# An attention kernel with PSUM banks given by name and its side work ordered behind the score copies

## The chip, the cores and the metric

The kernel runs on one core of a Trainium2 chip. The metric is device time in microseconds (us) of one execution; three executions of the kernel before took 2622.65, 2625.44 and 2630.11 us, median 2625.44. Five engines work in parallel, each through its own instructions in order: PE (TensorE, matrix products into PSUM), DVE (VectorE), ACT (ScalarE), POOL (GpSimd) and SP, which here only issues DMA transfers. In the profile PEld is PE's load of weights.

## The reference

Two batches of 2048 tokens with 2048 features each, all in fp32:

```python
xn = layernorm(x)
qkv = xn @ Wqkv + bqkv                      # q, k, v of 512 features, one head
attn = softmax(q @ k.T / sqrt(512))
a = (attn @ v) @ Wo + bo
r = xn @ Wq_w.T                             # router, 16 features
gate = softmax of the top 16 of r @ keys.T, spread over 64 experts
z = (xn @ A_w.T), 64 experts of rank 8, each times its gate
out = x + a + 2 * (z @ B_w.T)
```

## The kernel before

Each fp32 operand is split into a high and a low part (`split_hi`, L121, a cast on ACT; `split_lo`, L124, a subtract on DVE), and a product is three matmuls over the parts (`PASSES`). Most products are done in the seven-product scheme of Strassen and Winograd, with steps P1 to P7 whose operands are sums of quarter blocks.

The work is staged. `first_block` transposes and normalizes the first 512 tokens (`turn`, L363 on) and makes their values; then come queries, keys and gated experts of the eight blocks of 512 tokens, four pairs of blocks in all. A block's last item makes its values (`values_out`, with DVE adds at L289, casts and subtracts, and stores `v_d<-vs`). Then attention runs from 1317.7 us to about 2010 us, and after it the output stage (`multiply`, L1408; `finish`, L1397) with 2688 matmuls.

Attention goes over four pairs of query blocks, with eight units of keys each. A unit has seven score steps, `score(g)` (L1131, six matmuls each), so a pair has 56. Their order is P1, P7, P2, P6, P4, P5 and P3, with the next unit's P1 ahead of P3 in the later pairs and after it in the first. P1's bank is copied by ACT into a further bank, U (`seed`, L1114), and then P2 adds on into P1's bank, P6, P5 and P3 into U's, and P4 into P7's. ACT copies the banks of P7, P2, P6 and P3 to SBUF (L1144, L1146, L1149, L1157); DVE adds P4 and P5 (L1151, L1154) and keeps the running maxima (`greatest`, L1100, L1103). All score banks come from one pool of seven PSUM banks, given in the order in which they are asked for (`acc`, L98); the eighth (`misc`) serves sums and spreads.

While one pair's scores are made, the pair before is weighted. `maxes` (L1166 to L1178) reduces the maxima of a block to `mq`, and `spread` (matmul L1188, copy L1192) puts them on all partitions. `soft(c)` subtracts them (L1203, DVE), takes the exponential (L1206, ACT), splits it into `ph` and keeps the sums L (L1214, L1216). `weigh(n)` multiplies `ph` by the values `vt` (L129), 64 groups of three matmuls for a block; at a block's end the sums are added over partitions by two matmuls (L1250, L1251), DVE takes the reciprocal (L1253) and multiplies the four banks by it (L1257), ACT adds the bias (L1258), and SP stores the result (L1259). The SBUF slots `ot` of that come from a ring of three of the four `mid` slots.

The order of the work is written out by hand. A table `side` deals side work to score steps: loads, splits and stores of later keys (`key_steps`: loads `kr<-k_d` at L860, casts and subtracts into `kst`, stores `kp_d<-kst`), of queries (`query_steps`, `query_load`, `query_split`, loads at L927) and of output weights (`combos`, L1288 to L1291). `key_load` (L975) loads `kt<-kp_d` four pairs of steps ahead of its score. A block `with behind("sp")` places what it holds, in the order of instructions, behind the instruction last recorded under that name. `begin` gives the step at which the weighting of each pair starts.

Of the kernel before, what the change touches and what calls it, by code (L numbers as in the profile page):

```python
# [62 lines left out]
def attn_ffn_kernel(ctx: ExitStack, tc, x, xT, wq, wv, wob, bqk, bv, bo, keysT, out):  # L63
# [31 lines left out]
    for tag, words in order:  # L95
        sb.tile([P, words], F32, name=f"slot{tag}", tag=tag, bufs=1)

    def acc():  # L98
        return psum.tile([P, T], F32, name="acc", tag="acc", bufs=7)

    def misc(shape=None):
        return psum.tile(shape or [P, T], F32, name="misc", tag="misc", bufs=1)
# [223 lines left out]
    def first_block():  # L326


        xs0 = [r_xs, r_xs, r_xs] + [big(j) for j in range(16, 21)]
        xn = [r_xh([P, 2, T], FR, "xh") for c in range(NCH)]  # L330
        rows, mv = {}, const.tile([P, NT, 2], F32, name="mv", bufs=2)
        rs = const.tile([P, NT], F32, name="rs")
        nm = const.tile([P, NT], F32, name="nm")

        def load(t, cols):
            rows[t] = [xs0[2 * t + c]([P, 1024], F32, "xs") for c in range(2)]
            for c in range(2):
                for h in range(1024 // cols):
                    a = h * cols
                    (nc.scalar if t == 0 and c else nc.sync).dma_start(  # L340
                        rows[t][c][:, a : a + cols],
                        x[t * P : (t + 1) * P, c * 1024 + a : c * 1024 + a + cols],
                    )

        def normal(t):
            st = const.tile([P, 4, 6], F32, name="st6", bufs=2)
            row_stats(mv[:, t, :], rows[t], 0, st)
            last["nm"] = nc.vector.tensor_scalar(nm[:, t : t + 1], mv[:, t, 0:1], -1.0, None, ALU.mult)
            rstd(rs[:, t : t + 1], mv[:, t, 1:2], 1)

        def scale(t):
            for n in range(4):
                c, h = divmod(n, 2)
                v = rows[t][c][:, h * 512 : (h + 1) * 512]
                if n < 3:
                    last["row"] = nc.vector.tensor_scalar(
                        v, v, mv[:, t, 0:1], rs[:, t : t + 1], ALU.subtract, ALU.mult
                    )
                else:
                    nc.scalar.activation(v, v, AF.Identity, bias=nm[:, t : t + 1])  # L360
                    last["mul"] = nc.scalar.mul(v, v, rs[:, t : t + 1])

        def turn(t, g0=0, g1=NCH // 4):  # L363
            sl = slice(t * P, (t + 1) * P)
            for g in range(g0, g1):
                pt = acc()
                for j in range(4):
                    c = 4 * g + j
                    k = (c % 8) * P
                    nc.tensor.transpose(pt[:, j * P : (j + 1) * P], rows[t][c // 8][:, k : k + P], ident)  # L370
                for part in range(2):
                    for j in range(4):
                        hi, lo = (xn[4 * g + j][:, a, sl] for a in range(2))
                        pj = pt[:, j * P : (j + 1) * P]
                        if part == 0:
                            split_hi(hi, pj)
                        else:
                            last["row"] = split_lo(lo, pj, hi)

        r_w0 = Ring(sb, "h0", "h1", "h2", "h3", "B25", "B26", "B32", "B33")  # L380

        def mul(ps, wh, t, c2):
            sl = slice(t * P, (t + 1) * P)
            for cc in range(2):
                c = 2 * c2 + cc
                product(
                    ps[:, :VH], lambda a: xn[c][:, a, sl], lambda b: wh[:, b, cc, :],
                    c == 0, c == NCH - 1,
                )

        N2 = NCH // 2
        warm = half(0)([P, T], mybir.dt.bfloat16, "warm")
        nc.vector.memset(warm, 0.0)
        pw = misc()
        for j in range(26):
            nc.tensor.matmul(pw, warm[:, :P], warm, start=True, stop=True)
        load(0, 512)
        normal(0)
        scale(0)

        wh = []

        def pieces(n):
            with behind("row", "nm", "mul"):
                while len(wh) < n:
                    eng = nc.gpsimd if 2 <= len(wh) < 5 else None
                    wh.append(wv_piece(0, len(wh), eng, ring=r_w0))

        pieces(1)
        turn(0, 0, 2)  # L410
        pieces(3)
        turn(0, 2, 4)
        pieces(5)
        load(1, 1024)
        ps = [acc() for t in range(NT)]
        for t in range(NT):
            if t + 1 < NT:
                with behind("row"):
                    normal(t + 1)
            if t == 0:  # L420
                pieces(6)
                load(2, 1024)
            for c2 in range(N2):
                if t + 1 < NT and c2 == 2:
                    scale(t + 1)
                if t == 0 and c2 == 4:
                    pieces(N2)
                    load(3, 1024)
                    constants()
                if t + 1 < NT and c2 == 6:  # L430
                    with behind("pe"):
                        turn(t + 1)
                mul(ps[t], wh[c2], t, c2)
        qr = router_in()
        for t in range(NT):
            with behind("row"):
                values_out(0, t, 0, r_ev, qr, ps[t])
        flush()
        ps = [acc() for t in range(NT)]
        for c2 in range(N2):  # L440
            w = wv_piece(1, c2)
            for t in range(NT):
                mul(ps[t], w, t, c2)
        for t in range(NT):
            values_out(0, t, 1, r_ev, qr, ps[t])
        return xn, qr
# [614 lines left out]
    r_L = half(6)  # L1061
    r_rl = half(7)
    r_ot = half(8)
    r_oo = mid(0, 1, 2)
    r_ll = mid(3)
    r_tp = mid(0, 1, 2, 3)
    r_ph = wide(0, 1, 2)
# [38 lines left out]

    bank, later = {}, []

    def seed(k):

        b = bank["U"] = acc()
        if k < 3:
            nc.tensor.matmul(b, bank["k"], bank["q"], start=True, stop=True)
        nc.scalar.copy(b, bank["P1"])  # L1114

    def score(g):

# [5 lines left out]
            bank["U0"] = bank["U"]  # L1123
        name = {"P2": "P1", "P4": "P7", "P6": "U0", "P5": "U0", "P3": "U0"}.get(step, step)
        if not more:
            bank[step] = acc()
        ps = bank[name]
        st, mv = kop.pop(g), qop[j, step]
        for d in range(2):
            for i, (a, c) in enumerate(PASSES):  # L1130
# [2 lines left out]
                    start=not more and d == 0 and i == 0, stop=d == 1 and i == 2,  # L1133
                    skip_group_check=more,
                )
        tt, copy = nc.vector.tensor_tensor, nc.scalar.copy
        if later:
            greatest(*later.pop())
        if step == "P1":
            bank["k"], bank["q"] = st[:, 0, 0, :], mv[0][:, 0, :]  # L1140
            if k < NKS:
# [2 lines left out]
            copy(unit(b1, m)[:, 1, :], ps)  # L1144
        elif step == "P2":
            copy(unit(b0, m)[:, 0, :], ps)  # L1146
            later.append((b0, m, 0))
        elif step == "P6":
            copy(S[b0, m][:, 1, :], ps)  # L1149
        elif step == "P4":  # L1150
# [2 lines left out]
        elif step == "P5":  # L1153
            tt(S[b1, m][:, 1, :], S[b1, m][:, 1, :], ps, ALU.add)  # L1154
            greatest(b1, m, 1)
        elif step == "P3":
            copy(S[b1, m][:, 0, :], ps)  # L1157
            later.append((b1, m, 0))
            if NKS <= k + 1 < NPAIR * NKS:
                seed(k + 1)  # L1160

# [31 lines left out]

    blocks = range(NB)

    def soft(c):

        if c >= NB * NK:
            return
        blk, k = blocks[c // NK], c % NK  # L1200
        u = S[blk, k // 2]
        if k % 2 == 0:
            nc.vector.tensor_tensor(  # L1203
                u, u, mbc[blk].unsqueeze(1).to_broadcast([P, 2, T]), ALU.subtract
            )
            nc.scalar.activation(u, u, AF.Exp, scale=SCALE)  # L1206
        e = u[:, k % 2, :]
        ph = r_ph([P, 2, T], FR, "ph")
        split_hi(ph[:, 0, :], e)
# [22 lines left out]
    def weigh(n):  # L1232
# [2 lines left out]
        blk, k = blocks[c // NK], c % NK  # L1235
        if d == 0:
            load_v(c + 3)
            soft(c + 2)
        if k == 0:
            av[blk, d] = acc()  # L1240
        vt, ph = vt_[c], pt_[c]
        product(
            av[blk, d], lambda a: vt[:, a, d * P : (d + 1) * P], lambda b: ph[:, b, :],
            k == 0, k == NK - 1,
        )
        if k == NK - 2 and d == 2:
            lh, ll = lsum[blk]
            with behind("pe"):
                pl = misc()
# [1 line left out]
                nc.tensor.matmul(pl, onesr, lh, start=False, stop=True)  # L1251
            rl_[blk] = r_rl([P, T], F32, "rl")
            nc.vector.reciprocal(rl_[blk], pl)  # L1253
        if k == NK - 1 and d == ND - 1:
            for d in range(ND):
                ot = r_oo([P, T], F32, "ot")
                nc.vector.tensor_tensor(ot, av[blk, d], rl_[blk], ALU.mult)  # L1257
                nc.scalar.activation(ot, ot, AF.Identity, bias=bv_sb[:, d : d + 1])  # L1258
                nc.sync.dma_start(oz_at(blk, 1, d), ot)  # L1259

# [200 lines left out]
    NW = 2 * NK * ND  # L1463
    total = NPAIR * NG1

    begin = [NG1 * (j + 1) + (9 if j in (0, NPAIR - 1) else 5) for j in range(NPAIR)]
    side = {}

    def deal(g, steps, every=1):
# [49 lines left out]
    deal(begin[0] - 8, [lambda c=c: load_v(c) for c in range(3)])  # L1519
    deal(begin[0] - 3, [lambda c=c: soft(c) for c in range(2)])  # L1520
    done = 0
    for g in range(begin[-1]):
        if g < total:
            score(g)
            if g % 2:
                key_load(g // 2 + 4)
        j, n = divmod(g, NG1)
        for st in side.get(g, []):
            with behind("sp"):
                st()  # L1530
        if j and j <= NPAIR:
            if n == 2:
                maxes(2 * j - 1)
            if n in (1, 4):
                with behind("pe"):
                    spread(2 * j - 2 + n // 4)
        if n == NG1 - 2 and j < NPAIR:
# [119 lines left out]
```

## Time and profile before

| | |
|---|---|
| three executions | 2622.65, 2625.44, 2630.11 us |
| profiled execution | 2625.36 us |
| its span | 2623.5 us |
| PE busy | 2592.8 us (99%) |
| DVE busy | 1921.8 us (73%) |
| ACT busy | 909.8 us (35%) |
| POOL busy | 528.2 us (20%) |
| moved by DMA | 608.09 MB, mean 232 GB/s |
| mean granted TensorE clock | 0.998 |

The span runs from the first to the last instruction; the execution's time has 1.9 us around it. A share is an average over all stages: DVE at 73% is nearly full in parts of attention and has room elsewhere. In the lists of waits an engine's idle time is put down to what ended it: the line and engine that released the instruction, or the DMA that landed. In a timeline a line is a group of like instructions: start, busy time, engine, line, operation, outputs and inputs, shape, number, and in brackets the idle time before the first with what ended it. A matmul of 128x128 by 128x512 starts every 0.227 us when PE works without a pause.

### The profile page before, as it was taken

Reading aid. Unit: us, or ns where it says so; the run is one execution under the profiler, and the core shown is the slowest. Engines: PE = TensorE matmul, PEld = TensorE weight load, DVE = VectorE, ACT = ScalarE, POOL = GpSimd, SP = SyncE. Lnnn points to the kernel's source line nnn. Section 1 sums busy time; section 2 is a strip of 40 time slices with the busy share of each in tenths; the row PEclk is TensorE's granted clock in tenths of the full one; section 3 lists DMA queues with packets and bytes.
Section 4 is the critical chain, followed back from the end, with each engine's and each line's share of the span. In section 5 each row is a group of like instructions: output and inputs, shape, how many; then the busy total and the mean of one; then the engine's idle time right before and its main releaser. Section 6 shows DMA issues by size and latency. Waiting matters only on the chain. (4 is left out here: it accounts for less than half of the span.)

```text
span 2623.5 us, 34496 instructions
## 1 busy us (share of the span) xinstructions
PE 2592.8 (99%) x12692; PEld 2186.1 (83%) x12692; DVE 1921.8 (73%) x2695; ACT 909.8 (35%) x1345; POOL 528.2 (20%) x318
## 2 busy tenths in 40 slices
PE   9999999999999999999989999999999999999999
PEld 8889888888888888888877887878878888888887
DVE  7567649867878677776758859678597776797775
ACT  4333223323332323343435436344264222332221
POOL 2312420001000010000000000000001665565664
PEclk9999999999999999999999999999999999999999
DMA  6767874668446683577899798899788555565542
GB/s 235 249 242 252 297 272 167 218 214 275 147 137 230 211 274 119 182 253 234 307 302 324 253 341 269 267 323 323 245 298 294 169 166 163 185 215 172 180 162 103
DMA packets 328954, 608.09 MB, mean 232 GB/s; under 512 B 27928, under 2 KB 150864, under 8 KB 328784
## 3 DMA queue, kind: packets, MB, share of 16 engines
q1 hardware_dynamic: 315824, 575.99, 65.0%
q10 hardware_dynamic: 12960, 29.89, 3.3%
q8 instruction: 100, 1.64, 0.3%
q14 instruction: 70, 0.57, 0.1%
HBM read 450.42 MB, written 155.35 MB: 231 GB/s over the span
## 5 line engine op out<-in xcount | busy, mean ns | idle before, releaser
L129 PE MATMUL acc<-t,pw 128*128 128x512 f32 x3024 | 693.7, 390 | 0.4 <-DVE pw L124 0.4
L129 PEld LDWEIGHTS acc<-t,pw 128*128 128x128 f32 x3024 | 565.4, 188 | 118.1 <-DVE pw L124 0.8
L1408 PE MATMUL acc<-wb,s 128*128 128x512 f32 x2688 | 609.4, 389 | 0.0
L1408 PEld LDWEIGHTS acc<-wb,s 128*128 128x128 f32 x2688 | 504.7, 188 | 104.6
L1392 POOL TENSOR_TENSOR xo<-xo,bo_bc 128x512 f32<-128x512 f32 x128 | 210.7, 1653 | 897.7 <-DMA vt<-v_d 605.5
L129 PE MATMUL acc<-ph,vt 128*128 128x512 f32 x1536 | 377.9, 390 | 4.5 <-DVE ot L1257 2.1
L1131 PE MATMUL acc<-qt,kt 128*128 128x512 f32 x1344 | 338.0, 393 | 14.3 <-ACT acc L1114 7.6
L129 PEld LDWEIGHTS acc<-ph,vt 128*128 128x128 f32 x1536 | 287.3, 188 | 68.4 <-DVE ot L1257 3.7
L1131 PEld LDWEIGHTS acc<-qt,kt 128*128 128x128 f32 x1344 | 252.7, 189 | 73.6 <-ACT acc L1114 8.4
L121 ACT CAST pw<-pw 128x1024 fp32r<-128x1024 f32 (+1 forms) x168 | 177.8, 1059 | 333.7 <-PE acc L129 250.2
L129 PE MATMUL acc<-xh,wh 128*128 128x512 f32 x1152 | 263.6, 390 | 0.0
L124 DVE TENSOR_TENSOR pw<-pw 128x1024 fp32r<-128x1024 f32 (+1 forms) x168 | 213.9, 1274 | 62.0 <-ACT pw L121 60.0
L129 PEld LDWEIGHTS acc<-xh,wh 128*128 128x128 f32 x1152 | 215.6, 188 | 44.9
L129 PEld LDWEIGHTS acc<-pw,t 128*128 128x128 f32 x2016 | 245.9, 188 | 2.1 <-DVE yv L768 0.8
L129 PE MATMUL acc<-pw,t 128*128 128x264 f32 x2016 | 246.7, 284 | 0.6 <-DVE yv L768 0.6
L121 ACT CAST s<-xz 128x1024 fp32r<-128x1024 f32 x112 | 118.0, 1054 | 368.4 <-PE acc L1408 298.7
L124 DVE TENSOR_TENSOR s<-xz,s 128x1024 fp32r<-128x1024 f32 x112 | 177.4, 1587 | 37.1 <-ACT s L121 37.1
L124 DVE TENSOR_TENSOR wh<-wu,wh 128x512 fp32r<-128x512 f32 x96 | 87.1, 924 | 91.0 <-ACT wh L121 90.9
L521 POOL TENSOR_TENSOR zt<-zt,g 128x512 f32<-128x512 f32 x24 | 39.8, 1668 | 503.3 <-DVE zt L520 183.8
L124 DVE TENSOR_TENSOR t<-xq,t 128x1024 fp32r<-128x1024 f32 x84 | 108.2, 1292 | 20.1 <-ACT t L121 19.7
L1397 DVE TENSOR_TENSOR xo<-xo,acc 128x512 f32<-128x512 f32 x128 | 86.8, 680 | 49.1 <-POOL xo L1438 20.3
L121 ACT CAST t<-xq 128x1024 fp32r<-128x1024 f32 x84 | 88.3, 1052 | 96.1 <-PE acc L129 44.5
(169 smaller groups left out, 2469.7 us busy)
## 6 DMA issues: line engine op xcount, KB each, us to landing
vt<-v_d SPq DMA_DIRECT2D x128, 512.0 KB, 5.4
kt<-kp_d SPq DMA_DIRECT2D x224, 256.0 KB, 5.6
pw<-sq_d SPq DMA_DIRECT2D x72, 512.0 KB, 3.9
xo<-in_x SPq DMA_DIRECT2D x128, 256.0 KB, 3.4
xz<-oz_d SPq DMA_DIRECT2D x64, 512.0 KB, 4.8
out_y<-xo SPq DMA_DIRECT2D x128, 256.0 KB, 2.4
pw<-in_wq SPq DMA_DIRECT2D x54, 512.0 KB, 3.9
wu<-in_wq SPq DMA_DIRECT2D x48, 512.0 KB, 5.8
```

What stands on the lines that cost most here:

```text
L121: return nc.scalar.copy(hi, src)
L124: return (eng or nc.vector).tensor_tensor(lo, src, raw(hi), ALU.subtract)
L129: last["pe"] = nc.tensor.matmul(ps, st(a_), mv(b_), start=first and n == 0, stop=end and n == 2)
L521: nc.gpsimd.tensor_tensor(zt, zt, gx[n], ALU.mult)
L1131: last["pe"] = nc.tensor.matmul(ps, st[:, d, a, :], mv[c][:, d, :], start=not more and d == 0 and i == 0, stop=d == 1 and i == 2, skip_gro ...
L1392: nc.gpsimd.tensor_tensor(xs, xs, bo_bc[q // (NB // 2 * NH), c], ALU.add)
L1397: nc.vector.tensor_tensor(xs, xs, ps, op)
L1408: nc.tensor.matmul(ps, st[a_][:, kk, sl], mv[b_], start=not more and kk == 0 and n == 0, stop=kk == ND - 1 and n == 2, skip_group_check=more,)
```

## The change

It has five parts.

1. PSUM banks have names. `acc(n)` is bank n of seven; without n, the banks go round in a list. In attention P1 has bank 4, P7 bank 6 and U bank 5 (0, 2 and 1 in every second unit of the first pair), and the weighting's four banks are 0 to 3. In `first_block` the transposes go round three banks. The matmul in front of the seed copy is made for two units and not three.
2. Side work is placed behind the last score copy (ACT) and the last score add (DVE) as well as behind SP's last recorded transfer.
3. At a block's end of weighting ACT copies each bank to SBUF as its product ends, and DVE multiplies there; the ring for it has four slots and not three. The sums over partitions and the reciprocal come at the last unit's second group, not at the third group of the unit before.
4. `soft` is traced in three parts (subtract; exponential; splits and sums), one with each of three groups of weighting.
5. The maxima of P2 and P3 are taken two score steps later or more; the second spread of a pair comes at step 4 with the first at step 2, not 1; the weighting of the second and third pair begins at step 6, not 5.

```diff
-    def acc():
-        return psum.tile([P, T], F32, name="acc", tag="acc", bufs=7)
+    banks = list(range(7))
+
+    def acc(n=None):
+
+        if n is None:
+            n = banks.pop(0)
+            banks.append(n)
+        return psum.tile([P, T], F32, name="acc", tag=f"acc{n}", bufs=1)
...
-                pt = acc()
+                pt = acc(g % 3)
...
-        ps = [acc() for t in range(NT)]
+        ps = [acc(3 + t) for t in range(NT)]
...
-        ps = [acc() for t in range(NT)]
+        ps = [acc(t) for t in range(NT)]
+        banks[:] = 4, 5, 6, 0, 1, 2, 3
...
-    r_oo = mid(0, 1, 2)
+    r_oo = mid(0, 1, 2, 3)
+    ot_ = {}
...
+    def maxima(g):
+
+        while later and later[0][0] <= g - 2:
+            greatest(*later.pop(0)[1:])
+
     def seed(k):
 
-        b = bank["U"] = acc()
-        if k < 3:
+        b = bank["U"] = acc(5 - 4 * (k < NKS and k % 2))
+        if k < 2:
             nc.tensor.matmul(b, bank["k"], bank["q"], start=True, stop=True)
-        nc.scalar.copy(b, bank["P1"])
+        last["copy"] = nc.scalar.copy(b, bank["P1"])
...
-            bank[step] = acc()
+            bank[step] = acc((4 if step == "P1" else 6) - 4 * (k < NKS and k % 2))
...
-        tt, copy = nc.vector.tensor_tensor, nc.scalar.copy
-        if later:
-            greatest(*later.pop())
+
+        def tt(*ops):
+            last["add"] = nc.vector.tensor_tensor(*ops)
+
+        def copy(*ops):
+            last["copy"] = nc.scalar.copy(*ops)
+
+        maxima(g)
...
-            later.append((b0, m, 0))
+            later.append((g, b0, m, 0))
...
-            later.append((b1, m, 0))
+            later.append((g, b1, m, 0))
...
-    def soft(c):
+    def soft(c, part=None):
+
 
         if c >= NB * NK:
+            return
+        if part is None:
+            for part in range(3):
+                soft(c, part)
             return
         blk, k = blocks[c // NK], c % NK
         u = S[blk, k // 2]
-        if k % 2 == 0:
+        if part == 0 and k % 2 == 0:
             nc.vector.tensor_tensor(
                 u, u, mbc[blk].unsqueeze(1).to_broadcast([P, 2, T]), ALU.subtract
             )
+        if part == 1 and k % 2 == 0:
             nc.scalar.activation(u, u, AF.Exp, scale=SCALE)
+        if part < 2:
+            return
...
-            soft(c + 2)
+        if d < 3:
+            soft(c + 2, d)
         if k == 0:
-            av[blk, d] = acc()
+            av[blk, d] = acc(d)
...
-        if k == NK - 2 and d == 2:
+        if k == NK - 1 and d == 1:
...
-        if k == NK - 1 and d == ND - 1:
-            for d in range(ND):
-                ot = r_oo([P, T], F32, "ot")
-                nc.vector.tensor_tensor(ot, av[blk, d], rl_[blk], ALU.mult)
-                nc.scalar.activation(ot, ot, AF.Identity, bias=bv_sb[:, d : d + 1])
-                nc.sync.dma_start(oz_at(blk, 1, d), ot)
+        if k == NK - 1:
+            ot = ot_[blk, d] = r_oo([P, T], F32, "ot")
+            nc.scalar.copy(ot, av[blk, d])
+            if d == ND - 1:
+                for d in range(ND):
+                    ot = ot_[blk, d]
+                    nc.vector.tensor_tensor(ot, ot, rl_[blk], ALU.mult)
+                    nc.scalar.activation(ot, ot, AF.Identity, bias=bv_sb[:, d : d + 1])
+                    nc.sync.dma_start(oz_at(blk, 1, d), ot)
...
-    begin = [NG1 * (j + 1) + (9 if j in (0, NPAIR - 1) else 5) for j in range(NPAIR)]
+    begin = [NG1 * (j + 1) + (9 if j in (0, NPAIR - 1) else 6) for j in range(NPAIR)]
...
+    last["add"] = last["dve"]
     for g in range(begin[-1]):
         if g < total:
             score(g)
             if g % 2:
                 key_load(g // 2 + 4)
+        else:
+            maxima(g)
...
-            with behind("sp"):
+            with behind("sp", "copy", "add"):
                 st()
...
-            if n in (1, 4):
+            if n in (2, 4):
```

## The prediction

> **What bounds the kernel now.** I read the busy shares first, then what PE waited for during attention, then the timeline at the longest of those waits, then the stretches after it with their DMA share.
>
> ```profile
> PE 2592.8 (99%) x12692; PEld 2186.1 (83%) x12692; DVE 1921.8 (73%) x2695; ACT 909.8 (35%) x1345; POOL 528.2 (20%) x318
> ```
>
> PE is the bound: span 2623.5 less 2592.8 busy leaves 30.7 us for any change that removes no matmuls. The change removes one of 12,712. So I ask only which of PE's waits go and which come. The waits on PE between 1317 and 2050 us (total, times, longest):
>
> ```profile
> PE acc L1131 <- ACT acc L1114: 7.6, 2, 7.4
> PE acc L1131 <- ACT sp L1157: 4.4, 6, 1.4
> PE acc L1131 <- DMA kt<-kp_d: 2.3, 4, 1.0
> PE acc L129 <- DVE ot L1257: 2.1, 2, 1.7
> PE acc L129 <- DVE ph L124: 1.9, 2, 1.3
> PE misc L1188 <- DVE mq L1178: 1.4, 3, 0.6
> ```
>
> One wait stands out: score matmuls behind the seed copy (L1114). The timeline there, with idle time and its releaser in brackets:
>
> ```profile
> 1317.75 1.54 PE L1131 MATMUL acc<-qt,kt 128*128 128x512 f32 x6
> ...
> 1320.99 0.40 ACT L121 CAST kst<-kr 128x256 fp32r<-128x256 f32 x1 [9.93 <-DMA kr<-k_d]
> ...
> 1326.65 1.05 ACT L121 CAST vs<-vs 128x264 fp32r<-128x264 f32 x3 [0.33 <-DVE vs L289]
> ...
> 1327.61 0.58 ACT L1114 COPY acc<-acc 128x512 f32<-128x512 f32 x1
> ...
> 1328.23 2.07 PE L1131 MATMUL acc<-qt,kt 128*128 128x512 f32 x4 [7.36 <-ACT acc L1114]
> ```
>
> The seed copy takes 0.58 us and its bank was full by 1319.5, but ACT stood 9.93 us at a cast of side work (kst) whose keys were still in flight; five more casts, DVE's subtracts between them and the last values' casts (vs) followed. Step P2 adds into the bank that the copy reads, so PE stands still 7.36 us. DVE reached the values' adds (L289) only at 1326.13, so the copy could not have overtaken much.
>
> ```profile
> core 0: us, PE busy (x) PEld busy (x) DVE busy (x) ACT busy (x) POOL busy (x), PEclk, DMA share, GB/s
> 1317.00:1340.00 23.00, 15.64 (x61) 12.45 (x60) 11.01 (x25) 6.77 (x16) 0.00 (x0) 0.78 0.71 230
> 1340.00:1360.00 20.00, 19.43 (x85) 15.59 (x84) 10.44 (x17) 7.04 (x15) 0.00 (x0) 1.00 1.03 345
> 1360.00:1380.00 20.00, 19.39 (x84) 15.25 (x83) 13.00 (x26) 8.12 (x18) 0.00 (x0) 1.00 1.03 358
> ```
>
> Two things: the granted clock drops to 0.78 in the stretch of the wait, and afterwards the DMA share is full.
>
> **What the Trainium skill says.** "TensorE: Matmul & The Clock Gate", Part 1: The HAM clock gate, says that a TensorE idle for a window of about 3.4 us falls back to half clock, and needs about as long of work to come back. The trace agrees: after the 7.36 us, 14 matmuls start 427 ns apart instead of 227. The same page, under "Architectural detail", calls ACT and DVE strict FIFO; the trace agrees (the copy behind the casts). "DMA: Bandwidth & Descriptors", Where 436 GB/s comes from, gives about 358 GB/s per core from HBM; the trace shows 345 to 363 in the full stretches. "Perfetto Trace Analysis", Optimizing Tensor Performance, Matmuls, wants matmul groups to rotate through banks so that evacuation overlaps; the 4.4 us behind L1157 are a rotation that comes round too early.
>
> **The change part by part.** I count a stall as the start-to-start distance of matmuls over the usual 0.227 us; the waits above are a little less.
>
> *Side work behind the score copies.* In the changed program's order on ACT, the casts of the values come first, then the seed copy, the copies of P7, P2 and P6, and only then the first kst cast. The adds of the values no longer stand behind kst work on DVE. Need: P2 is due 13 matmuls after the first score, 13 x 0.227 = 2.95 us. Supply: P1 ends 1.4 us in, and the three casts of values ahead (about 0.4 us each, fed by adds 0.37 us apart) end near 1.9; the copy's 0.58 us ends at 2.5 to 2.7. So the wait should vanish: excess 7.53 us, plus 14 x (427 - 227) ns = 2.8 us cold clock, **-10.3 us**. The kst cast then comes after 1323, when its keys (landed 1320.99) are there. Cost elsewhere: a cast that lands behind a copy is at most one score step, 1.36 us, later; what it feeds is a pair away.
>
> *What comes back.* The first pair is nearly DMA-bound. From 1317 to 1425 the queues moved 35.5 MB; at 355 to 363 GB/s that is 98 to 100 us. PE needs 108 less its stalls (10.3, 3.2 for keys kt<-kp_d, 1.2 others), about 93. A pair pulled in by 10.3 us therefore collides with its own loads: 98.5 - 93.3 = 5.2 us of kt waits against 3.2 now, **+2.0**. But the first 20 us, where DMA stood partly idle, could absorb some, and landing is uneven: bounds 0 and +6; I take **+2.5**.
>
> *Named banks.* P7 now has a bank of its own whose last reader is the DVE add of P4, not one that ACT has just copied out (L1157). The six stalls there (0.88, 0.46, 1.57, 0.70, 0.58, 1.15) sum to 5.3. P2 still needs the seed copy, which sits behind the same late ACT work but is due six matmuls later: I keep 70%, **-3.7** (0 to -5.3). One seed matmul less: -0.2. In the first block the transposes' third group reuses a bank whose casts must be done: +0.5 at most, counted below. The last values' banks are now 4, 5, 6, 0, and the first P1 waits for the first of their adds, which ends before it: nothing, because the last three tiles' own matmuls cover it; 0.4 us, one add, if not.
>
> *Weighting's banks copied out.* The four multiplies (L1257, 678 ns) keep their length with an SBUF operand: other DVE work on SBUF (L124, 128x512) takes 692. ACT gets 32 copies of about 0.6 us, 19 us in all, and is 35% busy; they are placed as each bank's product ends. Behind a copy on ACT wait score copies, and behind those PE; but each copy is ready when it comes up, as its product has just ended. PE now waits for a 0.6 us copy and not for the reciprocal (3.35 us) and a queue of DVE multiplies. With a fourth slot, the multiply that stood 2.62 us for the store of three before is free. Stalls at L1257: 1.83 + 0.57 + 0.18 + 0.37 = 2.95; **-2.5** (0 to -3).
>
> *Softmax in three parts, maxima later, spread at 4 with 2.* Same instructions, other order. DVE has no room at the start of a pair: it was busy 22.9 of the 25 us from 1400 to 1425, and will be. The stalls at L1188 (2.2 us) and at ph (2.6 us) I leave; the later begin of pairs 1 and 2 packs the weighting tighter. The mid slots, shared by stores of keys and by divisors, may add 0.2 to 1 us per pair. **+2** for all new waits (bounds -3 and +6).
>
> Sum: -10.3 + 2.5 - 3.7 - 0.2 - 2.5 + 2 = -12.2. Against the profiled execution's own 2625.36 (span 2623.5 and 1.9 around it) that gives 2613.2; the median of the runs, 2625.44, is the same within 0.1. Order ahead of the attention and in the output stage is the same on DVE, SP and PE, so nothing is counted there.
>
> **Rivals.**
>
> *A, the first pair is DMA-bound and all of the pull-in returns as kt waits* (6 us or more, first pair; the small gains of 6 partly kept). For it: DMA share 1.02 to 1.05 from 1340 to 1425 and four kt waits already. Against: 98 to 100 us of transfers in 108. Time: 2625.4 - 10.3 + 8 - 3 = 2620.
>
> *B, every wait goes and nothing comes back*: 2625.4 - 10.3 - 3.2 - 5.3 - 3 = 2603.6. Against: saturated DMA and a DVE with no room at pair starts.
>
> *C, slower: the new copy of a bank waits for its slot.* The slot (mid ring, four, shared with kst, queries and sums) is free when an earlier store has landed, 4 to 8 us after issue by other stores here. ACT stands at that copy, score copies queue behind it, and PE behind those. Eight blocks: it eats the 12 us from 1.5 us a block, and is 0.3% slower from 2.5. At 3.5 us a block: 2613 + 28 = 2641. Against: where I followed the order, the slot's last store is some 57 matmuls (12.9 us) earlier.
>
> *D, the change doesn't do it:* the seed copy still waits, now for DVE's adds or a late bank, and only small gains remain: 2623.
>
> **How the numbers follow.** 0.3% of this kernel, 7.9 us, is about what measurement can tell from no change: the limits are 2617.5 and 2633.3. My forecast (2607 to 2617) has 0.55, B 0.15, A 0.17, D 0.06, C 0.07. Faster: 0.55 + 0.15 = 0.70; same: A and D, 0.23; slower 0.07. The range leaves out C, part of D and the far end of B, under 0.2: 2604 to 2622.
>
> **What would show it.** Right: the wait behind the seed copy is gone and the clock of the stretch from 1317 to 1340 is 1.00; the waits on kt<-kp_d in the first pair are 4 to 8 us instead of 2.3; the waits behind L1157's successor and the multiply of ot are below 1.5 us together; ACT is busy 19 us more. Wrong: kt waits above 10 us (A); ACT waiting for DMA oz_d<-ot or kp_d<-kst at the new copy (C); new stalls at mq or ph above 5 us, as DVE's order in the weighting was not followed instruction by instruction for every block.

## The result

The changed kernel takes 2610.49 us (median of six executions, 2608.14 to 2613.55) against 2625.43 us for the kernel before (six executions, 2619.66 to 2630.11): a ratio of 0.9946, 95% interval 0.9931 to 0.9961, or 14.9 us less. The forecast was 2613.2 us with a range from 2604 to 2622. The profiled execution took 2613.24 us, its span 2611.4 us.

The busy shares of the changed kernel:

```profile
PE 2590.1 (99%) x12691; PEld 2185.3 (84%) x12691; DVE 1906.9 (73%) x2696; ACT 923.5 (35%) x1377; POOL 537.8 (21%) x318
```

PE is busy 2.7 us less than before (2592.8 us) in a span 12.1 us shorter: it was mostly waits that went. What PE waited for between 1300 and 2050 us (total, times, longest):

```profile
PE acc L1144 <- DMA kt<-kp_d: 2.6, 2, 1.8
PE acc L135 <- DMA vt<-v_d: 1.5, 2, 1.0
PE misc L1206 <- DVE mq L1196: 1.3, 2, 0.8
PE misc L1206 <- ACT ph L127: 0.7, 1, 0.7
PE acc L1144 <- ACT sp L1154: 0.5, 1, 0.5
PE acc L135 <- ACT ot L1283: 0.4, 1, 0.4
PE acc L1144 <- ACT acc L1127: 0.3, 1, 0.3
...
```

The seed copy's 7.6 us (now L1127) are 0.3, the 4.4 us behind the score copies 0.5 and the 2.1 us at ot 0.4. The 1.9 us that the weighting waited for ph are gone; 0.7 us put down to ph stand at a spread. The waits on values (vt, 1.5 us) are new. The timeline at the first scores:

```profile
1319.95 1.22 DVE L295 TENSOR_TENSOR vs<-acc,xv 128x264 f32<-128x264 f32 x3 [2.14 <-PE acc L135]
1320.47 1.15 ACT L127 CAST vs<-vs 128x264 fp32r<-128x264 f32 x3 [5.30 <-DVE vs L295]
...
1320.85 1.54 PE L1144 MATMUL acc<-qt,kt 128*128 128x512 f32 x6
...
1322.45 3.79 PE L1144 MATMUL acc<-qt,kt 128*128 128x512 f32 x16
1322.65 0.57 ACT L1127 COPY acc<-acc 128x512 f32<-128x512 f32 x1 [1.03 <-PE acc L1126]
```

DVE adds the values at once, ACT casts them, and the seed copy ends at 1323.22 us, 2.37 us after the first score began (expected: 2.5 to 2.7, due at 2.95). The scores go on without a gap. The stretches after it:

```profile
core 0: us, PE busy (x) PEld busy (x) DVE busy (x) ACT busy (x) POOL busy (x), PEclk, DMA share, GB/s
1317.00:1340.00 23.00, 22.52 (x116) 18.97 (x114) 13.38 (x28) 8.57 (x19) 0.78 (x1) 1.00 1.02 340
1340.00:1360.00 20.00, 18.19 (x72) 14.29 (x71) 12.67 (x25) 7.11 (x15) 0.00 (x0) 0.91 1.04 353
1360.00:1380.00 20.00, 20.00 (x89) 16.31 (x89) 12.79 (x25) 8.59 (x19) 0.00 (x0) 1.00 1.02 357
```

The first 23 us now have the full clock and a full DMA. I split the two profiled executions by the first score and the first output matmul:

| stage | before | after | difference |
|---|---|---|---|
| up to the first score | 1317.75 us | 1320.85 us | +3.1 |
| attention | 692.49 us | 675.38 us | -17.1 |
| output stage | 613.30 us | 615.23 us | +1.9 |

The 3.1 us ahead of attention can't be put down to the change: two runs below whose order there is that of the kernel before (the second part alone, the third part alone) reach their first score at 1321.07 and at 1317.42 us. The 1.9 us in the output stage are two waits of PE on DVE's splits of its operands, at 2328.6 and 2351.6 us, which the kernel before doesn't have; no run asks for their cause. Within attention I add up the excess of every matmul: its start-to-start distance from the one before it, less the usual distance for its shape. The sum was 31.0 us and is 14.1, 16.9 less, so it accounts for the gain in attention (17.1):

| late for | before, us | after, us |
|---|---|---|
| seed copy | 7.9 | 0.4 |
| slow clock after a wait | 2.8 | 1.8 |
| score copy (P7's bank) | 5.3 | 0.6 |
| keys kt (DMA) | 3.2 | 2.9 |
| ot | 3.0 | 0.6 |
| ph, with an add ahead of it | 2.6 | 0.8 |
| mq | 2.2 | 1.6 |
| values vt (DMA) | 0 | 1.9 |
| all smaller | 4.1 | 3.5 |

### The profile page after: what moved, and what is told of

Its sections match the earlier page's. It is cut to its first block, busy times and chain, and to the rows that moved or that the text cites. A ratio compares the mean times of both kernels' runs of the same rounds, so it can differ in the third digit from the quotient of the medians.

```text
span 2611.4 us, 34504 instructions
## 1 busy us (share of the span) xinstructions
PE 2590.1 (99%) x12691; PEld 2185.3 (84%) x12691; DVE 1906.9 (73%) x2696; ACT 923.5 (35%) x1377; POOL 537.8 (21%) x318
## 5 line engine op out<-in xcount | busy, mean ns | idle before, releaser
L1422 POOL TENSOR_TENSOR xo<-xo,bo_bc 128x512 f32<-128x512 f32 x128 | 223.0, 1751 | 874.7 <-DVE ph L130 587.9
L130 DVE TENSOR_TENSOR s<-xz,s 128x1024 fp32r<-128x1024 f32 x112 | 169.4, 1514 | 42.8 <-ACT s L127 42.8
L130 DVE TENSOR_TENSOR wh<-wu,wh 128x512 fp32r<-128x512 f32 x96 | 80.8, 859 | 97.5 <-ACT wh L127 97.5
```

What stands on the lines that cost most here:

```text
L130: return (eng or nc.vector).tensor_tensor(lo, src, raw(hi), ALU.subtract)
L1422: nc.gpsimd.tensor_tensor(xs, xs, bo_bc[q // (NB // 2 * NH), c], ALU.add)
```

## The experiments

All ratios are to the kernel before on the same chip. Stage times are those of each run's profiled execution.

### The second part alone

The kernel before, with its score copies and adds recorded and:

```diff
+    last["add"] = last["dve"]
...
-            with behind("sp"):
+            with behind("sp", "copy", "add"):
```

> The kernel before with the second part alone: side work is placed behind the last score copy and add. My theory: the 7.4 us wait behind the seed copy came from the order on ACT's and DVE's queues, so it goes with the cold clock after it (-10.3 us), the first pair's key loads give 1 to 3 us back, and the stalls behind L1157 and L1257 stay: 2617 us (2615 to 2620). Rival, that the named banks are what freed the seed copy: the wait stays near 7 us and the time at 2623 to 2626.

Measured: 2621.04 us, ratio 0.9979 (0.9970 to 0.9987). Attention took 686.7 us, 5.8 less than before. PE's waits there:

```profile
PE acc L1131 <- ACT sp L1141: 5.4, 4, 2.2
PE misc L1194 <- DVE mq L1184: 3.1, 3, 1.8
PE acc L129 <- DVE ot L1263: 3.0, 2, 2.3
PE acc L1131 <- DMA kt<-kp_d: 2.6, 3, 1.4
PE acc L129 <- DMA vt<-v_d: 1.0, 1, 1.0
PE acc L1131 <- DVE qt L124: 0.2, 1, 0.2
```

The wait behind the seed copy is gone altogether, in a kernel without named banks: the rival falls, and the order on the queues was the cause. The edit changes ACT's order and DVE's at once; no run separates the two. The time missed my range all the same, as nearly half of the 10.3 us came back, and not from DMA alone. By the sums of excess (31.0 then, 25.2 now) mq has 1.6 us more, kt 0.7, ot 0.7, the score copies 0.7, vt 1.1. My reading, which no run tests, is that PE arrives sooner at other things that are late.

### The change without its second part

```diff
-            with behind("sp", "copy", "add"):
+            with behind("sp"):
```

> The changed kernel without its second part: side work is placed behind SP's last transfer alone. My theory: the wait of some 7 us behind the seed copy and the slow matmuls after it come back, +10.3, less 1 to 2 us of key waits: 2619 us (2617 to 2622). Rival, that banks and the copying out do it: 2610.5, no wait above 1 us at the seed copy.

Measured: 2617.39 us, ratio 0.9967 (0.9954 to 0.9980), so the part is worth 5.5 us (by the ratios) to 6.9 us (by the medians) in place, little more than the intervals can tell. The timeline at the first scores:

```profile
1321.82 0.40 ACT L127 CAST kst<-kr 128x256 fp32r<-128x256 f32 x1 [10.10 <-DMA kr<-k_d]
...
1325.54 1.11 DVE L295 TENSOR_TENSOR vs<-acc,xv 128x264 f32<-128x264 f32 x3
...
1326.03 2.93 PE L1144 MATMUL acc<-qt,kt 128*128 128x512 f32 x6 [7.43 <-DVE vs L295]
```

ACT again stands 10.10 us at a cast whose keys are in flight, and DVE reaches the values' adds only after it. With named banks the wait (7.43 us) falls one step earlier than in the kernel before: the first P1 itself needs a bank from which DVE must add the values.

### The first, the third, and both together

Banks by name in the kernel before, the multiplies still from PSUM:

```diff
-        b = bank["U"] = acc()
-        if k < 3:
+        b = bank["U"] = acc(5 - 4 * (k < NKS and k % 2))
+        if k < 2:
...
-            bank[step] = acc()
+            bank[step] = acc((4 if step == "P1" else 6) - 4 * (k < NKS and k % 2))
...
-            av[blk, d] = acc()
+            av[blk, d] = acc(d)
```

> The kernel before with the first part alone: banks by name, and the weighting's four banks still multiplied by DVE straight from PSUM. My theory: the six stalls of P7 behind the copy L1157 (5.3 us) go, but a block's next products now need the same bank that DVE has yet to multiply, about 1.5 us at each of seven block changes, and the seed wait stays: 2631 us (2621 to 2640). Rival, that the fixed names cost the weighting nothing: 2621.

Measured: 2630.84 us, ratio 1.0019 (1.0009 to 1.0029). From PE's waits in attention:

```profile
PE acc L1138 <- DVE vs L295: 7.9, 1, 7.9
...
PE acc L135 <- issue: 2.7, 2, 2.5
...
PE acc L135 <- ACT wb L127: 1.8, 1, 1.8
PE acc L1138 <- DVE sp L1158: 1.7, 1, 1.7
```

The wait at the first scores stays (7.9 us). The six waits of P7 are gone (0.2 us left behind a score copy), and naming costs 5 us by the medians all the same. The profile shows part of that: new waits that it puts down to ot, wb and the issue in the weighting, to DVE's adds at the score banks (2.5 us), and longer ones on mq. They leave attention, with the wait ahead of its first score, some 2.9 us longer; another 3.1 us of the profiled execution (2631.42) lie ahead of attention, where the two runs named above differ by 3.6 us with the same order.

The third part alone in the kernel before (with its ring of four and the later place of the sums):

```diff
-        if k == NK - 1 and d == ND - 1:
-            for d in range(ND):
-                ot = r_oo([P, T], F32, "ot")
-                nc.vector.tensor_tensor(ot, av[blk, d], rl_[blk], ALU.mult)
+        if k == NK - 1:
+            ot = ot_[blk, d] = r_oo([P, T], F32, "ot")
+            nc.scalar.copy(ot, av[blk, d])
+            if d == ND - 1:
+                for d in range(ND):
+                    ot = ot_[blk, d]
+                    nc.vector.tensor_tensor(ot, ot, rl_[blk], ALU.mult)
```

> The kernel before with the third part alone: ACT copies the weighting's banks out, DVE multiplies in SBUF; banks still come from one pool. My prediction's step: only the waits on ot go, -2.5 us: 2623.5 (2622 to 2625). Rival, that banks which come free earlier also take away the waits of P7 and P1 behind L1157: 2618 (2616 to 2620). The seed copy's wait stays near 7 us in both.

Measured: 2620.22 us, ratio 0.9980 (0.9972 to 0.9988), between the two figures and outside both ranges. The waits on ot are gone, and so are those on ph (1.9 us); those behind the score copy fell from six (4.4 us) to three (3.7), those on mq grew from 1.4 to 3.0, and the seed copy's wait was 8.8 us in the profiled execution.

Both together in the kernel before, the two edits above in one:

```diff
+            av[blk, d] = acc(d)
...
+            nc.scalar.copy(ot, av[blk, d])
```

> The kernel before with the first and third parts together: named banks, and the weighting's banks copied out by ACT. Alone, naming cost 5 us and copying out gained 5. If they only add, 2625.5. My theory: copying out takes away what naming cost, since a named bank is then free 0.6 us after its product ends, so naming's own gain at P7 shows: 2618 (2615 to 2621), with waits on the score copies below 2 us and the wait at the first scores near 7 us.

Measured: 2616.79 us, ratio 0.9965 (0.9952 to 0.9978). PE's waits in attention:

```profile
PE acc L1139 <- DVE vs L295: 8.1, 1, 8.1
PE misc L1196 <- DVE mq L1186: 4.2, 3, 2.7
PE acc L1139 <- DMA kt<-kp_d: 2.2, 3, 1.0
PE acc L135 <- ACT ot L1264: 1.3, 1, 1.3
```

Alone the parts moved the median by +4.9 and -5.4 us; together by -8.9, where the sum of the two is -0.5. Naming needs the copying: beside it, the named banks save some 3.5 us, about what the intervals can just tell, and alone they cost 4.9. The copying pays without naming too. The wait at the first scores is 8.1 us, so named banks and copying together do not remove it.

### The change without its third part

The edit of the third part the other way round, with the ring of three and the sums a unit earlier:

```diff
-    r_oo = mid(0, 1, 2, 3)
+    r_oo = mid(0, 1, 2)
...
-        if k == NK - 1 and d == 1:
+        if k == NK - 2 and d == 2:
...
-            nc.scalar.copy(ot, av[blk, d])
...
-                    nc.vector.tensor_tensor(ot, ot, rl_[blk], ALU.mult)
+                nc.vector.tensor_tensor(ot, av[blk, d], rl_[blk], ALU.mult)
```

> The changed kernel without its third part: DVE multiplies from PSUM, ring of three, sums a unit earlier. My theory: with named banks the next block waits for DVE's multiplies, about 1.5 us at each of seven block changes: 2621 us (2613 to 2630), and waits on ot are 5 us or more. Rival, that the copying out is worth only what the waits at ot were before, 2.4 us: 2613.

Measured: 2627.87 us, ratio 1.0007 (0.9999 to 1.0014). Without this part the time can't be told from that of the kernel before: the part is worth 16 us (by the ratios) to 17 us (by the medians) in place. That lies inside my wide range, but well above my figure of 2621. Two places in its timeline show how:

```profile
1672.74 0.69 DVE L1283 TENSOR_TENSOR ot<-acc,rl 128x512 f32<-128x512 f32 x1 [4.48 <-DMA oz_d<-ot]
...
1673.49 0.73 PE L135 MATMUL acc<-ph,vt 128*128 128x512 f32 x2 [2.38 <-DVE ot L1283]
```

```profile
1910.01 3.35 DVE L1279 RECIPROCAL rl<-misc 128x512 f32<-128x512 f32 x1
...
1914.26 1.87 DVE L1283 TENSOR_TENSOR ot<-acc,rl 128x512 f32<-128x512 f32 x3
...
1915.03 0.77 PE L135 MATMUL acc<-ph,vt 128*128 128x512 f32 x1 [2.33 <-issue]
```

In the first, the fourth multiply waits 4.48 us until the store that used its slot has landed, and its bank, which the next block needs, stays taken. In the second the reciprocal and the multiplies behind it hold the banks; the profile names the issue, but the matmul starts 0.77 us after DVE's first multiply began, when a bank comes free. That execution was one of its shortest (2622.57 us), so the median holds more than these lines show.

### The fourth and the fifth part

The change with softmax traced whole:

```diff
-        if d < 3:
-            soft(c + 2, d)
+            soft(c + 2)
```

> The changed kernel without its fourth part: a block's softmax step is traced whole with the first of its weighting groups. My theory: the waits on ph come back, some 2.6 us as in the kernel before: 2613 (2611 to 2616). Rival, that three parts change nothing that PE waits for: 2610.5.

Measured: 2612.28 us, ratio 0.9952 (0.9936 to 0.9968). The time lies between the two figures and tells nothing: its interval covers most of the change's own. The waits decide: those of the weighting on ph did not come back (0.9 us at a spread, as in the change, which has 0.7). Within what can be told the part is worth nothing, and my theory of its mechanism fell.

The change with the old maxima, spread and begin:

```diff
-        while later and later[0][0] <= g - 2:
+        while later:
...
-            if n in (2, 4):
+            if n in (1, 4):
...
-    begin = [NG1 * (j + 1) + (9 if j in (0, NPAIR - 1) else 6) for j in range(NPAIR)]
+    begin = [NG1 * (j + 1) + (9 if j in (0, NPAIR - 1) else 5) for j in range(NPAIR)]
```

> The changed kernel without its fifth part: maxima at the next score step, first spread at step 1, weighting of the second and third pair from step 5. My theory: the waits on mq are as long in both traces (2.2 and 2.5 us), so the part is worth nothing: 2610.5 (2608 to 2613). Rival, that the later maxima keep DVE free for the adds that PE waits for: 2615 or more, with waits on mq above 4 us.

Measured: 2615.49 us, ratio 0.9961 (0.9947 to 0.9975). The waits on mq are four and 4.4 us in place of two and 1.3. The intervals of this run and of the change overlap, but the profile shows the rival's sign: the part most likely saves some 4 to 5 us beside the others, and my figure (worth nothing) fell. Its three edits were not separated.

### Is the first pair bound by DMA?

The change with less to move there:

```diff
-    for n in range(3):
-        keys(8 + n, 5 + 14 * n, 14 * n)
+    for n in range(2):
+        keys(8 + n, 12 + 14 * n, 7 + 14 * n)
...
-        (11, NG1 + 6), (12, NG1 + 18), (13, NG1 + 48), (14, 2 * NG1 + 9), (15, 2 * NG1 + 19)
+        (10, NG1 + 27), (11, NG1 + 6), (12, NG1 + 18), (13, NG1 + 48), (14, 2 * NG1 + 9), (15, 2 * NG1 + 19)
```

> The changed kernel with less to move in the first pair: of three blocks of later keys that are made there, one is made in the second pair and the others start seven steps later. If the waits on kt in the first pair (2.6 us, and 1.6 us of cold clock after them) come from a full DMA, they go for the most part: 2607 (2605 to 2609.5). If they come from the place of the loads in SP's queue, or if the second pair pays for it on DVE: 2610 to 2613.

Measured: 2612.61 us, ratio 0.9959 (0.9944 to 0.9974). Its waits and two stretches of the first pair:

```profile
PE acc L1144 <- ACT acc L1127: 6.4, 4, 2.1
PE misc L1206 <- DVE mq L1196: 2.8, 2, 2.5
PE acc L135 <- DMA vt<-v_d: 1.9, 1, 1.9
PE acc L135 <- ACT ot L1283: 1.1, 1, 1.1
PE acc L1144 <- DVE qt L130: 0.2, 1, 0.2
```

```profile
1360.00:1380.00 20.00, 20.00 (x90) 16.57 (x89) 11.80 (x23) 8.48 (x18) 0.00 (x0) 1.00 0.98 322
1380.00:1400.00 20.00, 20.00 (x90) 16.57 (x89) 12.23 (x16) 9.33 (x14) 0.00 (x0) 1.00 0.99 319
```

No wait on kt is left, DMA runs at 320 and not 357 to 366 GB/s, and the first pair, up to its first spread, takes 89.4 us in place of 91.4. So less traffic takes the key waits away. The edit also moves the loads to other places in SP's queue, so by itself it doesn't show that the amount alone counts. The kernel gains nothing: the side work now meets the queries' sums on DVE, ACT's casts wait for it (3.43 us at one place), and the seed copy behind them is late four times. (The profiled execution, 2617.03 us, was one of the longer ones of this run.)

The other way round, 12 more transfers in the first pair, failed as an experiment:

```diff
+            if 8 <= g < 44 and g % 3 == 0:
+                nc.sync.dma_start(more_d[g], q_d[0][0])
```

> The changed kernel with 12 more transfers of 512 KB from one scratch array to another, queued on SP at score steps 9 to 42 of the first pair; they feed nothing. At 355 GB/s they take 17.7 us. If the first pair is DMA-bound, most of that comes out as waits on kt there: 2622 (2618 to 2628). If the key waits are only a matter of place in the queue and DMA has room: 2610.5 to 2614.

Measured: 2613.54 us, ratio 0.9949 (0.9936 to 0.9961). The trace has these transfers between 111 and 167 us: nothing tied them to their place in the order, and they were issued long before attention. The run says nothing of the first pair.

### Two attempts at a better version

The change with the queries' second load in halves:

```diff
-    for g, st in zip((2, 6, 8, 12, 16, 18), query_steps(1, r_qs)):
+    qs_ = query_steps(1, r_qs)
+    for g, st in zip((2, 6, 8, 18, 20), qs_[:3] + qs_[4:]):
         deal(g, [st])
+    deal(10, [lambda: qs_[3]((0,))])
+    deal(14, [lambda: qs_[3]((1,))])
```

> The changed kernel with the second load of the next pair's query parts in two halves (score steps 10 and 14 in place of 12), its sums and stores two steps later. If the wait on kt at 1349.3 us (2.0 us and 1.6 us of cold clock) comes from those four loads queued ahead of the key loads, it goes: 2607.5 (2606 to 2610). If it comes from the amount that the first pair moves, it only moves: 2610.5.

Measured: 2611.01 us, ratio 0.9943 (0.9930 to 0.9956). The two-microsecond wait and the slow clock after it are gone, but kt waits add up to 3.0 us of start-to-start excess as before, and 1.4 us at the queries' sums are new; waits on ph also grew, from 0.7 to 2.5 us. The wait moved, as the amount of traffic would have it.

With the second spread at step 8 as well:

```diff
-            if n in (2, 4):
+            if n in (2, 8):
                 with behind("pe"):
-                    spread(2 * j - 2 + n // 4)
+                    spread(2 * j - 2 + n // 8)
```

> As the run with the split load, and a pair's second spread at step 8 in place of 4, so that PE doesn't wait for the maxima that DVE has yet to reduce; the second block is not weighted until half a pair later. My theory: two waits at that spread (0.6 and 0.8 us) go and the others stay: 1.5 us below the run with the split load alone, 2606 (2604 to 2609). Rival: DVE's work is what is late, and the wait comes up at the next weighting group instead: no gain over it.

Measured: 2609.66 us, ratio 0.9938 (0.9925 to 0.9950), the shortest time and the shortest attention (674.5 us) of all runs. Of the two waits that the later spread was meant to remove, the one at a second spread is gone, and the other, which stands at a pair's first spread, is still 0.8 us. The run beats the kernel before; against the change, 0.8 us is less than the intervals can tell.

## Why the prediction was right, and where it was not

**The total.** The forecast was -12.2 us; the medians give -14.9, the two profiled executions -12.1, of which -17.1 in attention. That -12.1 meets the forecast is luck: attention gained some 5 us more than forecast, and the other two stages, where nothing was counted, lost 5.0 in that execution. The forecast's terms were all of attention, so I hold them against its sums of excess (-16.9): seed copy and its slow clock, forecast -10.3, measured -7.5 with 2.8 of slow clock, -10.3; what comes back from the first pair's keys, forecast +2.5, measured +1.5 (kt 0.3 less; 1.8 of slow clock, nearly all behind one kt wait); P7's bank, forecast -3.7, measured -4.7; ot, forecast -2.5, measured -2.4; the rest, forecast +1.8 with the seed matmul, measured -1.1 (ph -1.8, mq -0.6, the smaller ones -0.6, vt +1.9). The term that was mis-sized most is the last: no large new wait appeared beyond vt, and mq did not grow.

**The mechanism of the largest term** is shown from both sides: the wait goes with the second part alone, and comes back without it. What the part saves is less than the term: 4.9 us alone and 5.5 to 6.9 in place, where the forecast's two terms (-10.3 and +2.5) make 7.8.

**The terms held only together.** In the whole change the named banks' term was -3.7 and measured -4.7, the copying's -2.5 and -2.4. As the worth of a part they mean nothing: named banks alone cost 4.9 us, and copying out is worth 5.4 alone and 16 to 17 beside named banks. The weak step is to price each edit at the waits of the kernel before. The prediction saw that the copy takes the reciprocal (3.35 us) and the multiplies out of PE's way, but priced that at the 2.95 us of the kernel before, where banks came from one pool; with fixed names these stand in the way of the next block's first products. Because the change brings both parts, the sum came out all the same.

**Mq, ph and the last two parts.** The prediction leaves the waits at mq and ph as they were and counts no gain for the fourth and the fifth part. That was wrong for the fifth: without it mq waits are 4.4 us instead of 1.3. The kernel before had 1.4, so the part mostly holds off what the other parts would bring. The fourth was indeed worth nothing that these runs can tell.

**What was to be seen.** Clock 1.00 from 1317 to 1340: yes. Waits on kt of 4 to 8 us in the first pair: no, 2.6. The full DMA share of the first 23 us (340 GB/s, 230 before) shows the room that the prediction named as a reason for less. Score copies and ot together below 1.5: yes, 0.9. ACT 19 us busier: no, 13.7, though the 32 new copies took 588 ns each, 18.8 us in all. New waits at mq or ph above 5 us: none. One reading was too quick: the slow clock after the wait of 7.36 us agrees with the passage that the prediction cites in the fall to half clock, but 14 matmuls at 427 ns are 6.0 us of work before full clock, not about 3.4. DVE's multiply takes 715 ns from SBUF and took 677 ns from PSUM, so the length that I kept was a little short.

**The rivals.** A (all comes back as kt waits) needed 6 us there, and the waits are not so long; that traffic sets them, as it held, is supported by the run with fewer transfers. B gave 2603.6; waits for DMA with 4.8 us of excess (kt and vt) remain. C did not happen: at the new copies ACT waited 8.7 us, 8.0 of them for PE, and no store is named. D is refuted by the timeline.

## What to carry to other kernels

A long wait on a busy engine can come from an instruction further up another engine's in-order queue that waits for a transfer; ask which side work stands ahead of the copy that the busy engine needs, and place it behind. Price edits to buffers in pairs: here fixed names for banks gained only where each bank was emptied at once, and cost where its release hung on a long chain. And expect part of any gain back at the next things that are late; here the largest single repair kept about half of its 10 us when made alone.

## What the runs showed of the hardware

A short wait can cost nearly as much again in clock. In the changed kernel PE was idle 1.81 us for keys (from 1349.71 us), and the clock fell only after it had gone on at 1351.52 (last columns: granted clock, DMA share, GB/s):

```profile
1350.00:1351.00 1.00, 0.00 (x0) 0.00 (x0) 0.20 (x1) 0.00 (x0) 0.00 (x0) 1.00 1.09 364
1351.00:1352.00 1.00, 0.48 (x2) 0.44 (x3) 1.00 (x2) 0.00 (x0) 0.00 (x0) 1.00 1.07 370
1352.00:1353.00 1.00, 1.00 (x5) 0.73 (x4) 1.00 (x3) 0.00 (x0) 0.00 (x0) 0.52 1.04 355
1353.00:1354.00 1.00, 1.00 (x4) 0.81 (x3) 1.00 (x3) 0.00 (x0) 0.00 (x0) 0.50 1.09 356
1354.00:1355.00 1.00, 1.00 (x4) 0.81 (x3) 1.00 (x2) 0.88 (x3) 0.00 (x0) 0.50 1.09 369
```

Eight matmuls at about 427 ns in place of 227 added 1.6 us. In the 14 profiled executions here, 10 of 19 waits with an excess of 1.9 to 3.0 us were followed by six or more such matmuls, the others by one or none. Of the waits from 1.2 to 1.9 us none was; all five above 7 us were, by 7 to 14. What sorts the 10 from the other 9 no run shows. So the idle window of about 3.4 us that the Trainium skill gives ("TensorE: Matmul & The Clock Gate", Part 1: The HAM clock gate) is no lower bound for a single wait here.
